# A graph attention kernel on one core: one batch's mask products and the copies into value blocks moved to the setup, and another listed order of the loop

## The chip, the cores and the metric

The kernel runs on one core of a Trainium2 chip, all in 32-bit floats. The metric is the device time of one execution in microseconds (us); lower is better. PE is the matmul engine (TensorE), DVE VectorE, ACT ScalarE, POOL GpSimd, SP SyncE, which issues most DMAs.

## The reference, cut to what matters

Sixteen batches (B) of 512 nodes with 512 features; a mask of 11 labels per pair of nodes, of which only the first 20 neighbours (NONGT) count; two directions d (the second with the mask transposed); 16 heads of 32.

```python
self_feat = concat([v, where(row_zero, 0, q)]) @ W_self.T + b_self
output = self_feat
for d in range(2):
    A = adj (d == 0) or its transpose (d == 1), first 20 neighbours
    cond, vb = A.sum(-1), A @ w_bias + b_bias
    kv = self_feat[:, :20]
    qh, kh = self_feat @ Wq[d].T + bq[d], kv @ Wk[d].T + bk[d]    # by head
    aff = where(cond > 0, einsum('bnhd,bmhd->bnhm', qh, kh) / sqrt(32), NEG) + vb
    w = softmax(aff)                                              # over the 20
    output += einsum('bnhm,bmf->bnhf', w, kv) through Wout[d] by head, + bout[d]
return v + relu(output)
```

## The kernel before, in words

**Setup (to about 97 us).** For all batches at once the setup works out the 20 neighbours' features, folds the query weights into the keys and the output weights into the values, and stores them in DRAM: keys in g_d (g1_d for batch 1), additive terms of the keys in cq_d, values in vw_d. The keys come in 22 bursts (n = 0 to 21, function keys): PE's matmuls, evictions into a stage "st" by ACT (L915) and DVE (L918), and, as soon as a stage is full, two stores by SP: a small one (L936, 76 KB) and a large one (L937, 1064 KB). There are four stage buffers, so a new stage waits for the stores of the fourth one before it. Between the bursts stand other pieces of the setup: masks and self_feat of batch 0 (L230), the clearing of the value blocks bd_d (L166, after bursts 8, 10, 12 and 14), and at n = 19 the two loads of batch 1's mask (adj, L141), after burst 19's stores. After the bursts come four loads of xn and the seeds.

**Value blocks.** For the last product (O) the values must lie in DRAM as blocks bd_d with zeros around them. Twelve DMAs (fill_block, L187, steps bl00 to bl11) copy rows of 128 bytes from vw_d into the cleared bd_d; each is 64 x 4 to 64 x 20 such rows. The loads vd (L162) read bd_d.

**The loop.** The loop is a software pipeline, unrolled. A table ORDER lists steps as "name±ahead"; the program goes through the table row after row (turn −1 to 17), and at turn t issues each step for batch t + ahead, if there is such a batch. Each engine gets its instructions in that order. The steps of one batch:
- loads (SP): Lx, Lxn, LG (keys), Lcq (L148, four DMAs), Lvd, Ladj; with PACE = 4 each load also waits for the instruction five earlier in the listing;
- seeds (ACT): sa writes the key terms cq into the bank pair ps_a (L476), sd the mask's sum into ps_d (L480), sc cq into ps_d again (L482);
- S1 to S7 (PE, L440): seven products of a Strassen-like scheme for the scores, 64 matmuls each, on sums y and z by POOL (Y and Z steps);
- t11 (ACT, L487) takes the first score tile out of ps_a, t12, f11 and so on (DVE, L492, L496) the others; then the softmax of four tiles: mx (DVE), sub (POOL L507), exp (ACT), sum, rec (DVE), nor (POOL L522), turn (DVE);
- F1 to F7 (PE, L292): seven products for the next batch's self_feat, on the banks ps_o; p and j (ACT, DVE) take them out;
- so (ACT, L533) puts self_feat into the banks ps_o, O0 and O1 (PE, L550) add the attention's output, oe (DVE, L560) ends it, st stores it;
- masks of the next batch: mul0 to mul10 (ACT, L363), one product of adj with the label's weight for each label, cnt (DVE, L369), flg (ACT), msum (DVE), sp (ACT).

For the last batch, other steps (P1 to P4, Oa to Oc) take the place of S and O.

S6 needs ps_a again after S1, so it waits until t11 has taken S1's result out. DMAs of SP and ACT are given completion counters, DMAHW0 to DMAHW7, in the order in which they are listed, whichever of the two engines issues them. In a list of the order, a row's "waits DMAHW3" means that this instruction waits until that counter has reached a value that the transfer given it before brings.

Of the kernel before, what the change touches and what calls it, by code (L numbers as in the profile page):

```python
# [14 lines left out]
NEG = -9000000000000000.0  # L15

ORDER = """
Z3+0 Z2+0 mul1+1 S2+0 mul2+1 Lx2+1 LG3+1 rec12-1 n22b-2 mul0+1 turn22-1 rb3-2 m22a-1 mul7+1 fu22+0
turn21-1 bl06+0 nor12-1 bl00+0 bl05+0 t11+0 S6+0 rb1-2 f11+0 bl02+0 P1+0 Lx3+1 Y3+0 u22a-1 turn12-1 e11+0
t12+0 mul9+1 bl09+0 mul10+1 bl11+0 so2-1 mul3+1 P4b-1 mul4+1 Lxn1+2 x22a-1 O0-1 Oa-1 mul6+1 O1-1 Lnz+1  # L20
k1+0 Z1+0 mul8+1 Lxn3+2 S7+0 Y4+0 mul5+1 sc+0 rb2-2 m22b-1 mx11+0 Ladj0+2 kv+1 oe2-1 flg+1 Lvd0+0 k2+0
oe3-1 rs0+2 S5+0 X1+1 sub11+0 LG1+1 oe0-1 F1+1 exp11+0 u22b-1 LG2+1 Lcq+2 ra0-2 v22a-2 rs2+2 t22+0 oe1-1
s22a-1 S4+0 bl01+1 msum+1 rs1+2 Z4+0 bl07+1 sum11+0 LG0+2 f22+0 Lx0+2 v22b-2 bl08+1 sA1-2 rs3+2 mx22+0
X2+1 f21+0 x22b-1 rm+2 p1+1 sp1+1 rec11+0 rb0-2 Ob-2 F6+1 bl04+1 bl10+1 nq+1 rst+2 P3+0 st1-1 ra3-1 bl03+1
nc+1 ra1-1 X3+1 Lxn0+3 sp0+1 S3+0 p2+1 P2+0 Ladj1+2 e21+0 mx21+0 sub22+0 exp22+0 Lvd3+0 nor11+0 nd+1 Oc-2
sub21+0 F7+1 rc0-2 exp21+0 X4+1 Lvd2+0 k3b+0 Lvd1+0 r22a-1 Lxn2+3 f12+0 F5+1 e12+0 sum22+0 p3+1 n22a-1
F2+1 F4+1 sd+1 st3-1 sA0-2 mx12+0 rec22+0 sum21+0 j3+1 sub12+0 rc2-2 nr+1 k0+1 st2-1 rec21+0 k3a+0 F3+1
turn11+0 j1+1 exp12+0 nor22+0 rc1-2 Lx1+2 p4+1 st0-1 s22b-1 nor21+0 sum12+0 sB0-2 j2+1 cnt+2 Y2+1 sa+1
S1+1 so3+0 P4a+0 rc3-2 ra2-1 sB1-2 so1+0 so0+0 r22b-1
"""  # L30
SOFT = 6
PACE = 4
# [3 lines left out]
def gat_kernel(  # L36
# [20 lines left out]
    nc = tc.nc  # L57
# [79 lines left out]
    def load_adj(b, i, ins=None):  # L137
        if i == 0:
            adjs[b] = load.tile([P, 4 * S, L], I32, tag="adj", name=f"adj{b}", bufs=1)
        to = adjs[b].rearrange("p (i v) l -> p i (v l)", i=2)  # L140
        behind(nc.sync.dma_start(to[:, i], adj[b, :, i]), ins)  # L141
# [29 lines left out]
    def blocks():  # L171

        bb = bd_d.rearrange("c b r e i g -> (c b) r e i g")
        vv = vw_d.rearrange("d c (b m) (e g) -> d (c b) m e g", m=NG, e=HL)
        for e in range(HL):
            for i in range(2):
                j = (e * S) // 32 + i
                for d in range(2):
                    lo = max(e * S + d * NG, 32 * j)
                    hi = min(e * S + (d + 1) * NG, 32 * j + 32)  # L180
                    if lo < hi:
                        m, r = lo - e * S - d * NG, lo - 32 * j
                        yield bb[:, r : r + hi - lo, e, i], vv[d, :, m : m + hi - lo, e]

    def fill_block(n):
        to, of = list(blocks())[n]
        nc.sync.dma_start(to, of)  # L187

    def ran(ins):
        done["all"].append(ins)  # L190
# [473 lines left out]
    with tc.tile_pool(name="setup", bufs=1) as sp, tc.tile_pool(name="ps_acc", bufs=4, space=PSUM) as acc["pool"]:  # L664
# [171 lines left out]
        with tc.tile_pool(name="setup_g", bufs=4) as sg:  # L836
# [137 lines left out]
            for n, runs in enumerate(bursts):  # L974
                for i in range(len(rest)):
                    if i < (4 if n == 0 else 1) or any(fc == 0 and (d, hg) == rest[0] for fc, hg, d, _, _ in runs):
                        key_rows(*rest.pop(0))
                keys(runs)
                for i in range(3 * n, min(3 * n + 3, 2 * C)):
                    bias_terms(i % 2, i // 2)  # L980
                if rest:
                    continue
                first = n if first is None else first
                for kind in plan[n - first] if n - first < len(plan) else ():
                    f, args = steps[kind].pop(0)
                    f(*args)
                if n == 5:
                    row_sums(0)
                if n in (8, 10, 12, 14):
                    clear_blocks(n // 2 - 4)  # L990
                if n == 7:
                    out_bias()
                if 8 <= n < 8 + C:
                    kv_bias(n - 8)
                if n == 12:
                    first_masks()
                if n == 13:
                    mask_count(0)
                if n == 14:
                    mask_flag(0)  # L1000
                    load_cq(0)
                if n in (14, 15):
                    for c in range(2):
                        self_flags(2 * (n - 14) + c)
                if n == 15:
                    mask_sum(0)
                    kv_copy(0)
                    row_sums(1)
                if n in (16, 17):
# [12 lines left out]
            while steps["s"]:  # L1022
                f, args = steps["s"].pop(0)
# [14 lines left out]
    with tc.manual_schedule():  # L1038
        banks = [bank(f"ps_o{c}", c) for c in range(C)]
        steps = {  # L1040
            "kv": kv_copy, "cnt": mask_count, "flg": mask_flag, "msum": mask_sum,
            "rm": row_mask, "rst": store_mask,
        }
        for c in range(C):
# [62 lines left out]

        def first(name):

            if name[:2] == "bl":  # L1110
                return (0,)
            if name in END:
                return (B - 1,)
            if name in NOT_END:
                return range(B - 1)
            if name[:2] in ("Lx", "rs", "rm", "La") or name == "Lnz":
                return range(3 if name[:3] == "Lxn" else 2, B)
            if name[0] in "FXpj" or name[:2] in ("LG", "Lc", "mu") or name in (
                "nd", "nc", "nq", "nr", "cnt", "flg", "msum", "sp0", "sp1", "kv"
            ):  # L1120
                return range(1, B)
            return range(B)
# [70 lines left out]
```

## Time and profile before

| | us |
|---|---|
| median of 3 runs | 596.72 (596.09 to 597.12) |
| profiled execution | 591.75, span 590.0 |
| loop's first score product (S1.0) starts | 97.38 |
| S7.1 (batch 1) starts | 146.94 |
| P1 of the last batch starts | 555.97 |

Rows of a timeline read: start us, duration us, engine, line, operation, out<-in, tile (partitions x elements), count, and in brackets the idle time before it and what ended it. "ACT s L487" as a releaser means that ACT's instruction of line 487 came last. Rows of DMA groups have the KB of one and the median us from issue to landing. Windows give, for a stretch, its length and each engine's busy time. q1 is the queue of SP's DMAs, q8 fetches PE's instructions. Line numbers are those of the kernel before; in the new kernel they are one lower up to about line 1000.

### The profile page before, as it was taken

The numbers are of one execution on the slowest core, as the hardware profiler recorded it, in microseconds if no ns is written. First come the engines' busy times: TensorE is split into PE (matmuls) and PEld (weight loads), VectorE is DVE, ScalarE is ACT, GpSimd is POOL, SyncE is SP. The second block draws the span as 40 slices with busy tenths as digits, with TensorE's granted clock in tenths as the row PEclk, the third lists the DMA queues.
The fourth block names the chain that finished last, engine by engine and source line by source line (L and its number), as shares of the span: only waits on it lengthen the run. The fifth ranks groups of instructions, "written<-read, shape, count | busy, mean of one in ns | idle before, by whom it ended". The sixth has DMA issues, their size and how long they took to land.

```text
span 590.0 us, 31439 instructions
## 1 busy us (share of the span) xinstructions
PE 560.5 (95%) x13980; PEld 437.4 (74%) x13980; DVE 433.7 (74%) x628; ACT 413.4 (70%) x890; POOL 427.8 (73%) x374
## 2 busy tenths in 40 slices
PE   8999999697999999998999999999999999999994
PEld 5443356586878787887888888877887777899983
DVE  0576571575878787877888787878787878788765
ACT  1344571786787878786878787878786868786622
POOL 2637945476687878786888887878787878888643
PEclk9999999898999999999999999999999999999997
DMA  8999999878766767766667776767666767652222
GB/s 292 380 396 370 322 316 373 222 180 239 190 222 180 222 192 227 199 209 159 228 196 223 195 222 192 220 172 228 188 215 183 219 185 212 202 175 87 70 93 73
DMA packets 102199, 127.88 MB, mean 217 GB/s; under 512 B 21457, under 2 KB 66545, under 8 KB 100017
## 3 DMA queue, kind: packets, MB, share of 16 engines
q1 hardware_dynamic: 100272, 123.73, 67.5%
q8 instruction: 110, 1.80, 1.3%
q0 software_dynamic: 672, 1.36, 1.0%
q10 hardware_dynamic: 1120, 0.79, 0.4%
q14 instruction: 25, 0.20, 0.1%
HBM read 85.97 MB, written 40.24 MB: 214 GB/s over the span
## 4 chain that ended last, share of the span: by engine, by line
PE 83%; POOL 5%; DMA 4%; issue 4%; DVE 2%; SPq 1%; ACT 1%; DVEq 0%; POOLq 0%; ACTq 0%
PE ps_o L292 30%; PE ps_a L440 22%; PE ps_d L440 15%; PE ps_o L550 8%; PE ps_k L798 3%; PE ps_a L456 1%; DMA ws_q<-in_wsT 1%; DMA vw_d<-v 1%; POOL st L924 1%; POOL cq_d L861 1%; SPq L148 1%; PE ps_kv L748 1%; DMA g_d<-st 1%; PE ps_d L456 1%; DMA xn<-in_xn 1%
## 5 line engine op out<-in xcount | busy, mean ns | idle before, releaser
L507 POOL TENSOR_TENSOR s<-s,top 128x640 f32<-128x640 f32 x63 | 80.5, 1277 | 68.8 <-DVE top L503 68.8
L363 ACT ACTIVATE prod<-adj,wb_sb 128x160 f32<-128x160 int32 x165 | 84.8, 590 | 13.3 <-POOL t L267 7.9
L522 POOL TENSOR_TENSOR s<-s,sum 128x640 f32<-128x640 f32 x63 | 79.8, 1278 | 12.3 <-DVE sum L518 12.1
L440 PE MATMUL ps_a<-y,z 128*32 128x152 f32 x1920 | 74.0, 301 | 13.1 <-issue 8.2
L292 PE MATMUL ps_o<-t,ws_s 128*32 128x246 f32 x1440 | 83.7, 370 | 0.0
L440 PEld LDWEIGHTS ps_a<-y,z 128*32 128x32 f32 x1920 | 64.1, 112 | 21.7 <-issue 18.7
L440 PE MATMUL ps_d<-g,z 128*32 128x152 f32 x1920 | 71.3, 293 | 0.3 <-issue 0.3
L511 ACT ACTIVATE s<-s 128x640 f32<-128x640 f32 x63 | 46.1, 732 | 36.1 <-POOL s L507 35.7
L292 PEld LDWEIGHTS ps_o<-t,ws_s 128*32 128x32 f32 x1440 | 56.0, 110 | 16.6
L440 PEld LDWEIGHTS ps_d<-g,z 128*32 128x32 f32 x1920 | 64.8, 110 | 2.8 <-issue 1.2
L292 PE MATMUL ps_o<-x,ws_v 128*32 128x246 f32 (+1 forms) x960 | 59.4, 373 | 0.3 <-issue 0.3
L560 DVE SCALAR_TENSOR_TENSOR o<-ps_o,x 128x512 f32<-128x512 f32 x60 | 38.4, 683 | 22.9 <-ACT cond L375 9.3
L492 DVE TENSOR_TENSOR s<-ps_a,both 128x640 f32<-128x640 f32 x45 | 37.1, 825 | 23.4 <-PE ps_a L440 23.1
L550 PE MATMUL ps_o<-wt,vd 32*32 32x256 f32 (+1 forms) x2176 | 49.3, 381 | 4.5 <-issue 2.6
L503 DVE TENSOR_REDUCE top<-s 128x32 f32<-128x640 f32 x63 | 51.2, 812 | 0.6
L515 DVE TENSOR_REDUCE sum<-s 128x32 f32<-128x640 f32 x63 | 50.2, 798 | 0.3 <-ACT s L511 0.3
L529 DVE STREAM_TRANSPOSE wt<-s 128x640 f32<-128x640 f32 x63 | 49.4, 802 | 0.0
L533 ACT COPY ps_o<-sf 128x512 f32<-128x512 f32 x64 | 36.6, 587 | 17.7 <-DVE sf L335 15.5
L292 PEld LDWEIGHTS ps_o<-x,ws_v 128*32 128x32 f32 x960 | 37.3, 110 | 13.3 <-issue 0.8
L550 PEld LDWEIGHTS ps_o<-wt,vd 32*32 32x32 f32 x2176 | 30.9, 105 | 19.3 <-issue 6.8
L496 DVE TENSOR_TENSOR s<-ps_d,s 128x640 f32<-128x640 f32 x45 | 36.9, 820 | 9.8 <-PE ps_d L440 9.2
L390 ACT COPY both<-add 32x160 f32<-32x160 f32 x128 | 41.1, 321 | 1.7
(283 smaller groups left out, 1228.0 us busy)
## 6 DMA issues: line engine op xcount, KB each, us to landing
g<-g_d SPq DMA_DIRECT2D x60, 304.0 KB, 3.8
g_d<-st SPq DMA_DIRECT2D x16, 1064.0 KB, 7.3
out_T<-o SPq DMA_DIRECT2D x60, 256.0 KB, 4.0
xn<-in_xn SPq DMA_DIRECT2D x56, 256.0 KB, 3.7
x<-in_xT SPq DMA_DIRECT2D x56, 256.0 KB, 3.6
adj<-in_adj SPq DMA_DIRECT2D x32, 440.0 KB, 4.6
vd<-bd_d SPq DMA_DIRECT2D x64, 64.0 KB, 3.4
nz<-nz_d SPq DMA_DIRECT2D x14, 256.0 KB, 3.8
```

Of the source, the lines that this page charges most:

```text
L292: nc.tensor.matmul(to[bass.ts(a, R), i] if wide else to[bass.ts(a, R), i, :, HK:], lhs, mov, start=wide and i == 0, stop=k == 1, skip_grou ...
L363: ran(nc.scalar.activation(new_prod(b)[:, :, l], adjs[b][:, :, l], AF.Identity, scale=wb_sb[:, l : l + 1]))
L390: ran(nc.scalar.copy(adds[b][bass.ts(2 * pg + hp, R), :, 2 * t : 2 * t + 2], add[bass.ts(2 * pg + t, R)]))
L440: nc.tensor.matmul(to[bass.ts(q, R)], rows[:, k, q // 2, bass.ds((2 * t + u) * R, R)], keys[:, k, q % 2], start=False, stop=k == 1, skip_g ...
L503: ran(nc.vector.tensor_reduce(tops[b, ij], flat(soft_tile(b, ij)), AX.X, ALU.max))
L507: ran(engine.tensor_sub(s, s, tops.pop((b, ij)).unsqueeze(2).to_broadcast([P, 4 * 2 * HL, NG])))
L511: ran(nc.scalar.activation(s, s, AF.Exp))
L515: ran(nc.vector.tensor_reduce(tops[b, ij], flat(soft_tile(b, ij)), AX.X, ALU.add))
L522: ran(engine.tensor_mul(s, s, tops.pop((b, ij)).unsqueeze(2).to_broadcast([P, 4 * 2 * HL, NG])))
L529: ran(nc.vector.transpose(wts[b][:, j, i], soft_t.pop((b, ij)).rearrange("p v h m -> p (v h m)")))
L550: nc.tensor.matmul(to, vds[b][r, j, e, i], w[:, :, bass.ts(block, 32)], start=False, stop=i == 1, skip_group_check=True,)
L560: ran(nc.vector.scalar_tensor_tensor(o, banks[q].rearrange("p (j n) -> p j n", j=2), 0.0, of_out(xs[b], hp, pg), ALU.max, ALU.add))
```

## The change

It has three parts. (1) The twelve copies into value blocks leave the loop and SP's queue: ACT issues them in the setup, three after each of the bursts 19, 20 and 21, and three after the last. (2) The two loads of batch 1's mask move from n = 19 to n = 15, ahead of three pairs of key stores on SP. (3) The table ORDER is replaced by another, which begins at another point of the row; batch 1's mask products, its F1 and most of batch 0's scores now stand in row −1. PE's steps in a steady row were F1 S4 F6 S3 F7 F5 F2 F4 F3 S1 S2 S6 O0 O1 S7 S5, and are F1 S4 S3 F6 F2 F7 F5 F4 F3 S1 S2 S6 O1 O0 S7 S5.

```diff
 ORDER = """
-Z3+0 Z2+0 mul1+1 S2+0 mul2+1 Lx2+1 LG3+1 rec12-1 n22b-2 mul0+1 turn22-1 rb3-2 m22a-1 mul7+1 fu22+0
...
+rs2+2 f22+0 flg+1 P3+0 Ladj0+2 oe1-1 ra0-1 sub11+0 fu22+0 p1+1 mx22+0 msum+1 Z4+0 n22a-1 st1-1 X2+1 S3+0
...
     def fill_block(n):
         to, of = list(blocks())[n]
-        nc.sync.dma_start(to, of)
+        nc.scalar.dma_start(to, of)
...
                     row_sums(1)
+                    load_adj(1, 0)
+                    load_adj(1, 1)
                 if n in (16, 17):
                     mask_spread(0, n - 16)
-                if n == 19:
-                    load_adj(1, 0)
-                    load_adj(1, 1)
+                if n > 18:
+                    for i in range(3):
+                        fill_block(3 * (n - 19) + i)
+            for n in range(9, 12):
+                fill_block(n)
             for j in range(4):
                 load_xn(2, j)
...
-        for n in range(len(list(blocks()))):
-            steps[f"bl{n:02d}"] = lambda b, n=n: fill_block(n)
...
-            if name[:2] == "bl":
-                return (0,)
```

ACT's queue from the end of the setup into the loop, before. L915 are evictions of the last key bursts, L480 and L476 the seeds sd and sa of batch 0, L363 the mask products of batch 1, L487 the step t11 of batch 0:

```order
L915 COPY st_1117<-ps_g(3, 3, 0, 0, 2)0_1107 128x2x8x19
L915 COPY st_1117<-ps_g(3, 3, 1, 1, 2)0_1139 128x2x8x19 [waits PE_49]
L480 COPY ps_d<-both_987 128x4x160 [waits DVE_49,PE_49,Activation_49]
L476 COPY ps_a<-cq_904 128x4x160 [waits DMAHW2_49,DMAHW1_49,DMAHW3_49,DMAHW0_49,Activation_49]
L363 ACTIVATE prod_1275<-adj_1104,wb_sb 128x160 [waits DMAHW6_49,DMAHW5_49,Pool_49]
L363 ACTIVATE prod_1275<-adj_1104,wb_sb 128x160 x3
L487 COPY s_11_1316<-ps_a 128x640 [waits DMASW2_49,DMASW3_49,DMASW1_49,DMASW4_49,DMASW0_49,DMASW5_49,PE_49,Activation_49]
```
The same place of the new kernel, a little shortened at its start (L914 evictions, L186 block copies, the first three of which stand ahead of these rows, L475 the seed sa):

```order
L914 COPY st_1120<-ps_g(3, 3, 0, 0, 2)0_1110 128x2x8x19
L186 DMA bd_d<-vw_d 64x20x32 [waits DMAHW2_49]
L186 DMA bd_d<-vw_d 64x4x32 [waits DMAHW4_49]
L186 DMA bd_d<-vw_d 64x16x32 [waits DMAHW5_49]
L914 COPY st_1120<-ps_g(3, 3, 1, 1, 2)0_1145 128x2x8x19 [waits PE_49]
L186 DMA bd_d<-vw_d 64x16x32 [waits DMAHW6_49]
L186 DMA bd_d<-vw_d 64x4x32 [waits DMAHW0_49]
L186 DMA bd_d<-vw_d 64x20x32 [waits DMAHW1_49]
L186 DMA bd_d<-vw_d 64x8x32 [waits DMAHW3_49]
L186 DMA bd_d<-vw_d 64x12x32 [waits DMAHW5_49]
L186 DMA bd_d<-vw_d 64x20x32 [waits DMAHW0_49]
L475 COPY ps_a<-cq_904 128x4x160 [waits DVE_49,PE_49]
```
Behind these stand L479 (sd), L486 (t11), L481 (sc) and only then the eleven L362 of batch 1. So t11 moved ahead of the mask products, and the evictions and the seeds moved behind block copies that wait on DMAHW counters. The same holds a row later: t11 of batch 1 stood behind four mask products of batch 2, and now stands ahead of all eleven.

SP's queue at the same time, before (L937 a large key store, L936 the small one ahead of it, L141 the loads of batch 1's mask):

```order
L937 DMA g_d<-st_886 128x2128 [waits DMAHW6_49]
L936 DMA g_d<-st_965 128x152 [waits DMAHW7_49,DVE_49,Activation_49]
L937 DMA g_d<-st_965 128x2128 [waits DMAHW0_49,DVE_49,Activation_49]
L936 DMA g_d<-st_1007 128x152 [waits DMAHW1_49,DVE_49,Activation_49]
L937 DMA g_d<-st_1007 128x2128 [waits DMAHW2_49]
L936 DMA g_d<-st_1050 128x152 [waits DMAHW3_49,DVE_49,Activation_49]
L937 DMA g_d<-st_1050 128x2128 [waits DMAHW4_49]
L141 DMA adj_1104<-in_adj 128x880 [waits DMAHW5_49]
L141 DMA adj_1104<-in_adj 128x880 [waits DMAHW6_49]
```
and in the new kernel (the stages st_965, st_1007, st_1050 and st_1117 of before are st_968, st_1010, st_1053 and st_1120 here):

```order
L936 DMA g_d<-st_886 128x2128 [waits DMAHW6_49]
L140 DMA adj_955<-in_adj 128x880 [waits DMAHW7_49]
L140 DMA adj_955<-in_adj 128x880 [waits DMAHW0_49]
L935 DMA g_d<-st_968 128x152 [waits DMAHW1_49,DVE_49,Activation_49]
L936 DMA g_d<-st_968 128x2128 [waits DMAHW2_49,DVE_49,Activation_49]
L935 DMA g_d<-st_1010 128x152 [waits DMAHW3_49,DVE_49,Activation_49]
L936 DMA g_d<-st_1010 128x2128 [waits DMAHW4_49]
L935 DMA g_d<-st_1053 128x152 [waits DMAHW6_49,DVE_49,Activation_49]
L936 DMA g_d<-st_1053 128x2128 [waits DMAHW0_49]
L935 DMA g_d<-st_1120 128x152 [waits DMAHW3_49,DVE_49,Activation_49]
L936 DMA g_d<-st_1120 128x2128 [waits DMAHW7_49,DVE_49,Activation_49]
```
The two loads moved ahead of three pairs of stores, and from st_1053 on the stores share the counters with ACT's block copies, which take numbers between them.

More of the change, by code (lines that the diff above doesn't have):

```diff
@@ L17 @@
 ORDER = """
-Z3+0 Z2+0 mul1+1 S2+0 mul2+1 Lx2+1 LG3+1 rec12-1 n22b-2 mul0+1 turn22-1 rb3-2 m22a-1 mul7+1 fu22+0
[L19 to L29, printed above, removed]
+rs2+2 f22+0 flg+1 P3+0 Ladj0+2 oe1-1 ra0-1 sub11+0 fu22+0 p1+1 mx22+0 msum+1 Z4+0 n22a-1 st1-1 X2+1 S3+0
+LG0+2 exp11+0 e12+0 sum11+0 ra3-1 f12+0 rec11+0 mx12+0 nd+1 nq+1 sub22+0 kv+1 X4+1 Lx0+2 X3+1 rs0+2 Lvd3+0
+Lvd2+0 Lvd1+0 F6+1 F2+1 p2+1 exp22+0 sum22+0 rb1-1 ra2-1 e21+0 rs3+2 k3a+0 Lxn2+3 nc+1 rs1+2 F7+1 v22b-2
+F5+1 st3-1 j1+1 rb3-2 nor11+0 f21+0 sub12+0 rb2-2 exp12+0 rm+2 p3+1 F4+1 rec22+0 sa+1 Ob-2 rst+2 P4a+0
+sA1-2 nr+1 Lxn0+3 mx21+0 k3b+0 sum12+0 j3+1 sp1+1 nor22+0 m22a+0 p4+1 F3+1 Oc-2 k0+1 S1+1 sp0+1 sd+1 Y2+1
+P4b+0 st0-1 rb0-2 Ladj1+2 sub21+0 s22b-1 rec12+0 S2+1 v22a-1 u22a+0 exp21+0 so3+0 Lcq+2 Lx1+2 turn11+0
+nor12+0 j2+1 t11+1 Z3+1 Z2+1 so2+0 sum21+0 m22b+0 rec21+0 sA0-2 turn12+0 P1+1 turn22+0 u22b+0 rc2-2 S6+1
+so1+0 Lx3+2 so0+0 k1+1 O1+0 f11+1 x22a+0 r22b-1 Lx2+2 s22a+0 rc0-2 nor21+0 Lxn3+3 sc+1 turn21+0 O0+0
+x22b+0 rc3-2 n22b-1 LG3+2 Y3+1 t12+1 Oa+0 mul3+2 mul7+2 Y4+1 S7+1 Lnz+2 P2+1 sB0-2 e11+1 cnt+2 oe3+0 LG1+2
+mx11+1 mul5+2 oe0+0 mul1+2 mul9+2 mul6+2 rc1-2 mul0+2 Z1+1 sB1-2 Lvd0+1 X1+2 mul2+2 mul10+2 oe2+0 S5+1
+Lxn1+3 k2+1 r22a+0 LG2+2 ra1+0 mul4+2 t22+1 F1+2 st2+0 S4+1 mul8+2
 """
```

## The prediction

> **What bounds the kernel now.** I read the page's shares first, then the windows by stage, PE's timeline at the loop's start, and then back through ACT and SP to what PE waits for there.
>
> ```profile
> PE 560.5 (95%) x13980; PEld 437.4 (74%) x13980; DVE 433.7 (74%) x628; ACT 413.4 (70%) x890; POOL 427.8 (73%) x374
> ```
> PE is busy for 95% of a span of 590.0 us, so what can be won is 29 us of idle PE and whatever PE did at a low clock. The windows (sum, PE, PEld, DVE, ACT, POOL, then granted clock, DMA share, GB/s) show where that lies: the whole first part of the loop, its two slow places, the thirteen steady rows, and the best of these.
>
> ```profile
> 97.38:146.94 49.56, 39.72 (x1000) 33.43 (x992) 26.89 (x34) 32.64 (x72) 31.20 (x26) 0.93 0.83 229
> 107.16:110.58 3.42, 2.83 (x48) 2.56 (x52) 0.82 (x1) 3.42 (x8) 0.00 (x0) 0.50 0.55 159
> 141.30:144.70 3.40, 3.40 (x76) 2.53 (x69) 2.30 (x4) 3.40 (x8) 3.40 (x4) 0.50 0.87 277
> 146.94:535.56 388.62, 382.18 (x10409) 318.01 (x10408) 316.15 (x429) 316.17 (x687) 315.46 (x260) 1.00 0.68 200
> 206.63:235.58 28.95, 28.95 (x805) 23.43 (x800) 24.33 (x33) 23.88 (x54) 23.96 (x20) 1.00 0.70 206
> ```
> From S7.1 on (146.94) PE is the bound: 382.18 of 388.62 us at full clock, with the others at some 316. Before that PE is idle for 9.8 of 49.56 us and gets half its clock twice. PE's timeline there, row by row:
>
> ```profile
> 97.38 2.25 PE L440 MATMUL ps_a<-g,sf 128*32 128x152 f32 x64
> 107.75 3.63 PE L440 MATMUL ps_a<-y,z 128*32 128x152 f32 x64 [5.08 <-issue]
> 112.42 0.85 PE L440 MATMUL ps_a<-y,z 128*32 128x152 f32 x20 [1.04 <-DVE s L492]
> 140.42 3.50 PE L440 MATMUL ps_a<-y,z 128*32 128x152 f32 x64 [3.73 <-ACT s L487]
> 143.85 3.17 PE L550 MATMUL ps_o<-wt,vd 32*32 32x256 f32 x128
> 262.31 2.75 PE L550 MATMUL ps_o<-wt,vd 32*32 32x256 f32 x128
> ```
> S1.0 starts at 97.38, S6.0 waits 5.08 us and S6.1 3.73 us. Each then runs at half clock (3.63 and 3.50 for 64 matmuls that take 2.25 elsewhere), and the O0 behind the second is slow too (3.17; 2.75 at 262.31). ACT shows why:
>
> ```profile
> 91.13 0.99 ACT L915 COPY st<-s_g(3, 3, 0, 0, 2)0_1107 128x608 f32<-128x608 f32 x2 [2.91 <-DMA g_d<-st]
> 92.75 0.42 ACT L915 COPY st<-s_g(3, 3, 1, 1, 2)0_1139 128x304 f32<-128x304 f32 x1 [0.63 <-PE s_g(3, 3, 1, 1, 2)0_1139 L900]
> 96.48 0.69 ACT L476 COPY ps_a<-cq 128x640 f32<-128x640 f32 x1
> 105.10 1.97 ACT L363 ACTIVATE prod<-adj,wb_sb 128x160 f32<-128x160 int32 x4 [7.93 <-POOL t L267]
> 106.98 0.67 ACT L487 COPY s<-ps_a 128x640 f32<-128x640 f32 x1
> ```
> The copy that S6.0 needs (t11.0, L487) stands behind four mask products of batch 1 (L363). These are put down to POOL, but POOL's t has nothing to do with them: what came at 105.0 is batch 1's adj, as SP's rows show (start, us of issue).
>
> ```profile
> 86.82 0.43 SPq L937 DMA_DIRECT2D g_d<-st  x1
> 87.39 0.34 SPq L936 DMA_DIRECT2D g_d<-st  x1
> 87.84 0.85 SPq L937 DMA_DIRECT2D g_d<-st  x1
> ...
> 89.97 1.19 SPq L937 DMA_DIRECT2D g_d<-st  x1
> ...
> 92.62 1.59 SPq L937 DMA_DIRECT2D g_d<-st  x1
> 94.27 2.44 SPq L141 DMA_DIRECT2D adj<-in_adj  x2
> ...
> 103.77 4.32 SPq L148 DMA_DIRECT2D cq<-cq_d  x4
> ```
> ```profile
> DMA packets 2970, 8.35 MB, mean 348 GB/s; under 512 B 377, under 2 KB 1601, under 8 KB 2326
> q1 hardware_dynamic: 2967, 8.30, 93.8%
> g_d<-st SPq DMA_DIRECT2D x5, 1064.0 KB, 8.6
> adj<-in_adj SPq DMA_DIRECT2D x2, 440.0 KB, 9.5
> g_d<-st SPq DMA_DIRECT2D x5, 76.0 KB, 7.2
> ```
> The last three rows are of 84 to 108 us, KB and median us from issue to landing. adj is issued at 94.27 and 95.5 and lands 9.5 later, at 103.8 and 105.0, through a queue that is 93.8% full of key stores.
>
> **The change, part by part.** *Gone from the start: 11.9 us.* t11.0 now stands ahead of batch 1's products, and t11.1 ahead of batch 2's, so neither waits for an adj. That removes 5.08 + 3.73 of waits, 3.63 − 2.25 = 1.38 and 3.50 − 2.25 = 1.25 of half clock, and 3.17 − 2.75 = 0.42 of O0: 11.86. The wait of 1.04 on DVE stays. What is late next for S6.0 are POOL's sums, the last piece of POOL in the chain of waits there:
>
> ```profile
> 103.82 1.19 POOL t L267
> ```
> They end by 105, before S1.0 starts by the next step. The eleven products (1.97 us for four, 5.4 in all) then run on an ACT that has 17 us idle in this stretch: nothing on PE's path. The 11.86 is an upper bound; the lower would be the first wait alone, 6.5.
>
> *New in the setup: twelve block copies on ACT.* Their own issues are cheap and their waits are not.
>
> ```profile
> L187 SPq DMA_DIRECT2D bd_d<-vw_d x12: 536/658/1601, 108.6 to 121.6; - x12
> ...
> DMA to landing us min/median/max: 3.0/3.6/5.0
> ```
> ```profile
> SPq L148 <- DMA adj<-in_adj: 2.2, 2, 1.3
> SPq L148 <- DMA g_d<-st: 2.0, 1, 2.0
> ```
> The last two rows decide the forecast. The cq loads read cq_d, which no adj and no g_d touches, and yet they wait for both: the first issues at 103.77, the moment the first adj lands. The transfers of SP and ACT share eight completion counters (DMAHW0 to 7 in the order) that go round in listed order, and an issue waits until the transfer eight places back has landed. On SP's end of the setup that cost PE nothing. On ACT it does, since ACT's evictions and the seeds of S1.0 are queued behind. By the listed order, third block waits for st_968's small store, fourth and fifth for the 1-MB stores of st_968 and st_1010, eighth for that of st_1053, twelfth for the eighth block.
>
> So in time: adj takes SP's place at 87.4, and the stores behind it issue 2.44 later than the rows above. st_968's small store: 87.39 + 2.44 + 7.2 = 97.0, then the third block issues (0.66), and the eviction that stood at 91.13 comes at 97.7. st_1010's big one: 89.97 + 2.44 + 8.6 = 101.0: the last eviction comes at some 102.5, not 92.75. st_1053's big one: 92.62 + 2.44 = 95.1, plus landing. Landings run from 4.2 to 9.6 in this stretch:
>
> ```profile
> L937 SPq DMA_DIRECT2D g_d<-st x5: 430/1055/1593, 86.8 to 98.2; - x5
> ...
> DMA to landing us min/median/max: 4.2/8.6/9.6
> ```
> I take 9.6, since 0.88 MB of adj now stand ahead of it: 104.7. Eighth block lands 3.6 later, 108.3; twelfth issues (0.66), then the seed (0.69): S1.0 at 109.7 in place of 97.38, **+12.3**. Bounds: 106 (landings of 7 and 3.0; the 4.2 was the first store into a queue not yet full) and 113 (9.6 and 5.0, and 2 us for stores that wait for their own counters), so +8.6 to +15.7. PE is then idle for most of 94 to 109.7, and after each of its two long waits of before it ran at half clock, for 1.25 and 1.38 more: **+1.3** (0 to 1.4). The blocks leave SP's queue in the loop (12 x 0.66 = 8 us of issue between 108.6 and 122.3); PE waited for none of these: nothing.
>
> *The steady rows: +0.5 (−2.3 to +2.5).* Six self_feat products in one row are the same matmuls, on the same four banks. PE's waits from 177 to 536:
>
> ```profile
> PE ps_a L440 <- issue: 3.2, 3, 1.6
> PE ps_o L550 <- issue: 2.6, 3, 1.0
> ...
> q8 instruction: 110, 1.80, 1.3%
> ```
> No wait on another engine is left to remove; 5.8 us are waits that the profile ascribes to nothing, in or right behind O0 and O1, of whose short matmuls PE uses up the most instructions per us (128 in 2.75, against 64 in 2.25). The 110 instruction fetches (16 KB each) fit them, and both orders have the same instructions ahead of each O. The Trainium skill ("Runtime: NRT & Kernel Launch", Instruction fetch mechanics) says that such fetches are mostly hidden, as a sequencer dispatches slower than its store fills; by it, these waits would come from the order and could go. No row here shows a fetch hidden or not, so this is a rival. What the new order can add is a wait for a sum that comes just late on POOL or DVE, which have about 5 us free in a row of 28.95: I put 0.04 us in each of 13 rows, and at most 0.19. *The tail* begins with P1, in the chain of waits:
>
> ```profile
> 555.97 4.13 PE ps_a L456 x117
> ```
> From there to the end of the span are 590.0 − 555.97 = 34.0 us, with the same steps in both: 0, ±0.7.
>
> The profiled execution took 591.75, the median of the runs is 596.72, so the 4.97 between them lie outside of these rows, and the difference is put on the median: 596.72 − 11.86 + 12.3 + 1.3 + 0.5 = **599.0 us**.
>
> **The rivals.** *The blocks are only issued (0.12):* if ACT's counters are free when it gets there, the twelve cost ACT 12 x 0.66 = 7.9 us, of which 2.91 + 0.63 lie in waits of ACT, so S1.0 comes 4.4 later: 596.7 − 11.9 + 4.4 + 0.5 = 589.8, faster. It decides if the eighth block issues before 98; against it are the two rows on SP.
> *The stores land sooner (0.18):* as the median, 8.6, and 3.0 for the block: S1.0 at 108.1 and no half clock on top, 596.1 to 597.4, about **no change**.
> *Blocks and stores share each DMA engine (0.08):* two blocks that go out beside a 1-MB store may have to let it pass. At the 348 GB/s of the window 1064 KB are 3.1 us, so the eighth block lands 6.7 after its issue: 602.1. For it: 3.0 to 5.0 were measured without such a store beside. The Trainium skill ("DMA: Bandwidth & Descriptors", Queues, rings and completion order) has a DMA engine turn between the queues packet by packet, and a block consists of many small rows. No trace of before has two busy queues.
> *The waits behind O go (0.05):* 599.0 − 5.8 = 593.2, if they are due to the order.
> *A wait in every row (0.03):* one like the 1.04 on DVE, thirteen times: +13.5, 612. The waits of the steady rows name no engine at all, against it.
>
> **How the numbers follow.** The forecast has 0.54, the rivals 0.12, 0.18, 0.08, 0.05 and 0.03. The range 594.5 to 603.5 takes in S1.0 from 106 to 113 (595.3 to 602.4) with a little of the steady rows' bounds, and the second and third rivals; it leaves out 0.12 + 0.05 + 0.03 = 0.2. About 0.2% (1.2 us) can be told from no change. Faster: 0.12 + 0.05 + 0.03 of the second rival = 0.20. Same: 0.15 of it and 0.05 of the forecast = 0.20. Slower: 0.49 + 0.08 + 0.03 = 0.60.
>
> **What would show it.** In the new profile, ACT's last two evictions (the line of 91.13 and 92.75) at about 98 and 102.5, block copies on ACT's queue that wait for g_d transfers, S1.0 at 109.7, half clock in it, no wait ahead of S6.0 and S6.1, S7.1 some 2 us later than 146.94, 13 rows in 389 us and a tail of 34. S1.0 before 104 would prove the step on counters wrong; rows that together differ by over 2.5 us would do so for the steady part.

## The result and the profile after

The changed kernel takes **622.38 us** (median of 4 runs, 620.68 to 624.02) against 596.84 us before (596.09 to 597.12): 1.043 times as long, 95% interval 1.0396 to 1.0463. Forecast were 599.0 us and a range up to 603.5. The direction was right; the forecast rise over the median of before was 2.3 us, the measured one 25.5.

The page of the profiled execution (620.68 us; before: 591.75):

```profile
span 618.9 us, 31420 instructions
PE 566.7 (92%) x13980; PEld 441.5 (71%) x13980; DVE 434.0 (70%) x628; ACT 416.3 (67%) x890; POOL 427.4 (69%) x374
q8 instruction: 110, 1.80, 1.2%
```
The span is 28.9 us longer. PE's timeline, from the last key burst to the first O, says where the start went:

```profile
104.04 0.62 PE L899 MATMUL s_g(3, 3, 1, 1, 2)0_1145<-khD,wq_sb 32*128 32x152 f32 x2 [10.78 <-ACT st L914]
...
109.63 1.87 PE L229 MATMUL ps_sf<-x,ws_v 128*32 128x246 f32 x32
115.32 3.87 PE L439 MATMUL ps_a<-g,sf 128*32 128x152 f32 x64 [3.82 <-ACT ps_a L475]
...
122.23 2.27 PE L439 MATMUL ps_a<-y,z 128*32 128x152 f32 x64
125.55 2.27 PE L439 MATMUL ps_a<-y,z 128*32 128x152 f32 x64 [1.04 <-DVE s L491]
...
151.82 2.76 PE L549 MATMUL ps_o<-wt,vd 32*32 32x256 f32 x128
```
S1.0 starts at 115.32 instead of 97.38 and runs at about half clock (3.87 us). After it nothing waits for a mask: S6.0 follows at 122.23 with no wait, and only the 1.04 on DVE is left. The windows of the first part and of the thirteen rows:

```profile
115.32:154.51 39.19, 38.15 (x997) 32.49 (x997) 25.29 (x32) 29.50 (x63) 26.73 (x23) 0.96 0.58 160
154.51:562.67 408.16, 386.79 (x10405) 324.75 (x10400) 316.14 (x430) 318.96 (x690) 316.51 (x262) 1.00 0.65 193
```
So the 28.9 us are +17.9 (S1.0 later) − 10.4 (39.19 instead of 49.56 from S1.0 to S7.1) + 19.5 (408.16 instead of 388.62 for the rows) + 1.8 (S7.14 to the end: 618.9 − 562.67 = 56.2 against 590.0 − 535.56 = 54.4). The tail from P1 on is as long as before (34.3 and 34.4 from the first matmul of P1).

Most of the last term is one wait of 1.66 us behind S7.14, like those in the rows. PE's waits in the rows are these, and the profile gives no engine for any of them:

```profile
PE ps_a L439 <- issue: 8.7, 8, 1.8
PE ps_o L549 <- issue: 5.7, 4, 1.9
PE ps_d L439 <- issue: 4.7, 7, 1.3
PE ps_o L291 <- issue: 1.9, 5, 0.6
```
That is 21.0 us, against 6.4 before, and PE's busy time in the rows grew by 4.6 (386.79 against 382.18 for the same work); the profile does not say why.

**ACT at the end of the setup.** Its queue shows the evictions (L914) and the seeds (L475, L479) between block copies:

```profile
89.68 13.20 ACTq L186 DMA_DIRECT2D bd_d<-vw_d  x3
102.99 0.68 ACT L914 COPY st<-s_g(3, 3, 0, 0, 2)0_1110 128x608 f32<-128x608 f32 x1 [13.43 <-DMA bd_d<-vw_d]
...
103.62 3.46 ACTq L186 DMA_DIRECT2D bd_d<-vw_d  x2
107.12 0.42 ACT L914 COPY st<-s_g(3, 3, 1, 1, 2)0_1145 128x304 f32<-128x304 f32 x1 [3.14 <-DMA bd_d<-vw_d]
107.15 7.32 ACTq L186 DMA_DIRECT2D bd_d<-vw_d  x6
114.57 0.70 ACT L475 COPY ps_a<-cq 128x640 f32<-128x640 f32 x1 [7.02 <-DMA bd_d<-vw_d]
```
The two evictions that were forecast for 98 and 102.5 come at 103.0 and 107.1, the seed at 114.57. The records of the DMA instructions say what held the copies between: the transfer whose counter a copy waits for, when that landed, when ACT issued the copy and how long the issue took, and when the copy landed (us):

```
copy      waits for               landed    issued  took    lands
sixth     first copy              106.52    106.55  0.53   109.54
eighth    st_1053's large store   106.24    107.85  0.68   113.77
twelfth   eighth copy             113.77    113.79  0.68
third     st_968's small store     97.41     97.43  5.45   107.50
fifth     st_1010's large store   103.14    103.62  2.78   108.93
tenth     st_1120's small store   108.70    109.86  2.93   116.14
```
The first three rows are the chain that ends last: ACT waits for the first copy, which landed 16.8 us after its issue at 89.68, then goes through the sixth copy, the eviction and the seventh to the eighth, and the twelfth waits for the eighth to land. The last three rows are long issues beside it: from 89.7 to 114.5 the twelve issues took 17.3 us in all, and ACT's waits ahead of issues 7.0. These issues ended just before the landings of 106.52 and 113.77 (at 106.40, and at 113.47 with the eleventh copy), so either of the two would have held ACT nearly as long. Why they were long no run shows.

The group of the block copies (ns to issue, then us from issue to landing):

```profile
L186 ACTq DMA_DIRECT2D bd_d<-vw_d x12: 537/670/5450, 89.7 to 113.8; - x12
...
DMA to landing us min/median/max: 3.0/6.0/16.8
```

### The profile page after: what moved, and what is told of

It reads as the page before. It is cut to its first block, busy times and chain, and to the rows that moved or that the text cites. A ratio compares the mean times of both kernels' runs of the same rounds, so it can differ in the third digit from the quotient of the medians.

```text
span 618.9 us, 31420 instructions
## 1 busy us (share of the span) xinstructions
PE 566.7 (92%) x13980; PEld 441.5 (71%) x13980; DVE 434.0 (70%) x628; ACT 416.3 (67%) x890; POOL 427.4 (69%) x374
## 4 chain that ended last, share of the span: by engine, by line
PE 82%; DMA 6%; issue 5%; DVE 2%; POOL 2%; ACT 1%; SPq 0%; ACTq 0%; DVEq 0%; POOLq 0%
PE ps_o L291 29%; PE ps_a L439 21%; PE ps_d L439 15%; PE ps_o L549 7%; DMA bd_d<-vw_d 4%; PE ps_k L797 3%; DMA ws_q<-in_wsT 1%; PE ps_a L455 1%; DMA g_d<-st 1%; PE ps_v L874 1%; POOL st L923 1%; PE ps_kv L747 1%; PE ps_d L455 1%; ACT st L914 1%; POOL rx L216 0%
## 5 line engine op out<-in xcount | busy, mean ns | idle before, releaser
L291 PE MATMUL ps_o<-t,ws_s 128*32 128x246 f32 x1440 | 86.2, 371 | 0.7 <-issue 0.7
L362 ACT ACTIVATE prod<-adj,wb_sb 128x160 f32<-128x160 int32 x165 | 80.6, 586 | 0.0
L439 PE MATMUL ps_d<-g,z 128*32 128x152 f32 x1920 | 73.6, 293 | 4.8 <-issue 4.7
L291 PEld LDWEIGHTS ps_o<-t,ws_s 128*32 128x32 f32 x1440 | 58.4, 110 | 18.8 <-issue 1.6
L510 ACT ACTIVATE s<-s 128x640 f32<-128x640 f32 x63 | 46.3, 735 | 30.1 <-POOL s L506 29.7
L291 PE MATMUL ps_o<-x,ws_v 128*32 128x246 f32 (+1 forms) x960 | 61.4, 373 | 1.2 <-issue 1.2
L336 ACT COPY sf<-ps_o 128x492 f32<-128x492 f32 x30 | 17.1, 570 | 61.8 <-PE ps_o L291 53.1
L514 DVE TENSOR_REDUCE sum<-s 128x32 f32<-128x640 f32 x63 | 51.0, 809 | 10.7 <-ACT s L510 10.6
L502 DVE TENSOR_REDUCE top<-s 128x32 f32<-128x640 f32 x63 | 49.4, 785 | 0.1
L291 PEld LDWEIGHTS ps_o<-x,ws_v 128*32 128x32 f32 x960 | 40.0, 110 | 11.7 <-issue 1.5
L549 PEld LDWEIGHTS ps_o<-wt,vd 32*32 32x32 f32 x2176 | 30.5, 104 | 24.0 <-issue 11.5
L408 POOL TENSOR_TENSOR z<-sf,z 128x512 f32<-128x512 f32 x30 | 39.0, 1299 | 5.6 <-DVE sf L238 4.5
```

The lines of the kernel that those rows point to most:

```text
L291: nc.tensor.matmul(to[bass.ts(a, R), i] if wide else to[bass.ts(a, R), i, :, HK:], lhs, mov, start=wide and i == 0, stop=k == 1, skip_grou ...
L362: ran(nc.scalar.activation(new_prod(b)[:, :, l], adjs[b][:, :, l], AF.Identity, scale=wb_sb[:, l : l + 1]))
L408: ran(nc.gpsimd.tensor_sub(t, one, two))
L439: nc.tensor.matmul(to[bass.ts(q, R)], rows[:, k, q // 2, bass.ds((2 * t + u) * R, R)], keys[:, k, q % 2], start=False, stop=k == 1, skip_g ...
L502: ran(nc.vector.tensor_reduce(tops[b, ij], flat(soft_tile(b, ij)), AX.X, ALU.max))
L510: ran(nc.scalar.activation(s, s, AF.Exp))
```

## The experiments

Two causes were to be tested, each against a rival. For the start, *counters*: ACT waits in its queue for the transfers that hold the copies' completion counters (rival: the key stores themselves come later, as the mask's loads stand ahead of them). For the rows, *fetch*: PE waits for its instructions, whose fetches are held up by other transfers, and the new table crowds eight loads around O, where PE uses up its instructions fastest (rival: the new order of the steps makes PE wait for other engines). The second came up only with this trace. Of the DMA records of the changed kernel, four fetches of PE's queue (16 KB each) and the wait of PE behind each, in us:

```
fetch starts, ends   PE idle from, to    at matmul number
186.15  187.06       186.89  188.72       2999
250.62  251.66       251.41  253.04       4653 = 2999 + 13.0 x 127.2
405.23  406.20       405.75  407.69       8596 = 4653 + 31.0 x 127.2
469.25  470.14       469.98  471.77      10250 = 8596 + 13.0 x 127.2
```
PE stops at multiples of 127 matmuls (with their 127 weight loads; one fetch of 16 KB each) and starts again 1.4 to 1.7 us after the fetch has ended. Counted from when PE enters the block of instructions before, the fetch begins about 0.96 us later in the rows of before and 1.87 in those of after (means over some 80 fetches; over 2 us in about 10% and 48% of them). At their pace, a block of 127 matmuls of S lasts 4.1 us, one of O 2.7, one of F 6.6. So a fetch that begins 1.87 us late, takes 1.1 (the mean of the 110) and leaves 1.4 until PE goes on needs an estimated 4.4 us, more than a block of S gives; with 0.96 it is 3.5. The share of the DMA engines' time that other transfers took, by tenths of a row from the start of O (mean over 13 or 14 rows, worked out from the same records):

```
kernel before      0.67 0.50 0.71 0.73 0.39 0.75 0.77 0.57 0.63 0.66
changed kernel     0.90 0.68 0.80 0.60 0.71 0.55 0.15 0.49 0.68 0.81
loads spread       0.27 0.08 0.61 0.54 0.64 0.82 0.79 0.96 0.90 0.37
copies at O        0.95 0.76 0.55 0.52 0.56 0.61 0.84 0.73 0.56 0.93
```
In the changed kernel it is 0.90 while O runs and 0.15 in the middle of the F products. The two lower rows are experiments told below. In each comparison the kernel before ran on the same chip, with medians from 593.9 to 596.3 us; the changed kernel ran only for the result. The rows of one kernel differ between executions: thirteen rows took 388.6 us in the profile of before, and 389.8 and 395.1 in those of two experiments that leave its loads in the rows as they are (the old table with the new setup, and the mask's loads alone). A difference of up to some 7 us in the rows of two profiles is no effect by itself.

**The copies on SP** (changed kernel):

```diff
     def fill_block(n):
-        nc.scalar.dma_start(to, of)
+        nc.sync.dma_start(to, of)
...
-                if n > 18:
-                    for i in range(3):
-                        fill_block(3 * (n - 19) + i)
-            for n in range(9, 12):
-                fill_block(n)
             for j in range(4):
                 load_xn(2, j)
+            for n in range(12):
+                fill_block(n)
```


> The new kernel with one edit: the twelve block copies are issued by SP, all of them behind the four xn loads at the end of the setup, and not by ACT between the bursts. Theory (counters): the late start of the loop is ACT waiting in its queue for the transfers that hold the copies' counters. Then S1.0 starts at 97 to 100 instead of 115.3, without the 1.6 us of half clock, S7.1 at about 137 instead of 154.5, and the median falls by 16 to 18, to 604 to 606. Rival (the stores themselves come later, because the mask's loads now stand ahead of them): S1.0 stays behind 108, the median above 614. Both expect the steady rows to stay at 31.4 us.

Measured: median 613.1 us (603.15 to 615.73), ratio to before 1.0206 (1.0085 to 1.0327). S1.0, in the timeline of its profiled execution (603.15 us):

```profile
98.65 2.25 PE L439 MATMUL ps_a<-g,sf 128*32 128x152 f32 x64
...
135.23 2.27 PE L439 MATMUL ps_a<-y,z 128*32 128x152 f32 x64 [2.52 <-POOL z L408]
137.44 2.76 PE L549 MATMUL ps_o<-wt,vd 32*32 32x256 f32 x128
140.13 1.24 PE L439 MATMUL ps_a<-y,z 128*32 128x152 f32 x32
```
The start is back at 98.65, at full clock, with the mask's loads where the change put them: it was the copies on ACT, not the stores. That ACT waited for counters is read from the table above; this run takes the long issues off ACT together with the waits, so it does not part the two. S7.1 came 3 us later than expected, since S6.1 now waits 2.52 us for POOL. The rows stay slow (405.9 us). The median fell by 9, not 16, a miss: the profiled execution was the shortest of four, and what made the others (611.0 to 615.73 us) longer no profile shows.

**The loads spread** (changed kernel, table only; the steps of PE, ACT, DVE and POOL stay in their order):

```diff
-... F6+1 F2+1 p2+1 exp22+0 ... so0+0 ... Lx3+2 ... Lx2+2 ... Lxn3+3 ... LG3+2 ... LG1+2 ... Lxn1+3 ... LG2+2 ...
+... F6+1 Lx1+2 F2+1 LG3+2 p2+1 exp22+0 Lx2+2 ... F7+1 LG1+2 ... st3-1 Lx3+2 ... nor11+0 Lxn3+3 ... F4+1 LG2+2 ... Lxn0+3 Lxn1+3 ...
```


> The new kernel with eight loads (Lx1 to Lx3, LG1 to LG3, Lxn1, Lxn3) moved in the table from the stretch of S1 to S5 around O to the stretch of the six F products; all compute steps stand as they did. Theory (fetch): PE's unexplained waits in the steady rows are instruction fetches held up by the crowd of loads. Then the rows go from 31.4 to 29.4 to 29.8, the waits from 21 us to under 5, and the median falls by 16 to 24, to 598 to 606, with S1.0 still at about 115. Rival (the new order of the compute steps makes PE wait for other engines): the rows stay at 31 or more, the median within 4 us of 622.

Measured: 602.42 us (600.38 to 603.94), ratio to before 1.0131 (1.0053 to 1.0208) instead of 1.043: 8.6 us over the kernel before, where the changed kernel was 25.5 over it. The window of the thirteen rows, and PE's waits in them:

```profile
154.28:545.05 390.77, 383.18 (x10405) 320.28 (x10400) 316.02 (x430) 319.73 (x690) 316.99 (x262) 1.00 0.65 200
```
```profile
PE ps_a L439 <- issue: 4.8, 5, 1.4
PE ps_o L549 <- issue: 1.9, 3, 0.8
PE ps_d L439 <- issue: 0.5, 1, 0.5
```
With the same steps in the same order the rows take 390.8 us instead of 408.2, and the waits 7.2 instead of 21.0. S1.0 stays at 115.1. The rival for the rows has fallen. The median came as expected; the rows (30.1 us each) and the waits stayed just above what was expected.

**Both edits** (the two diffs above together). 

> Both edits together: copies on SP behind the xn loads, and the eight loads moved to the F stretch. Theory (counters and fetch, independent of each other): S1.0 at 97 to 100, rows at 29.4 to 29.8, median 580 to 588, faster than the kernel before by 9 to 16 us. Rival (either cost is something else): above 600.

Measured: 594.8 us (593.29 to 597.05), ratio 0.9997 (0.996 to 1.0033): no different from before, and a miss by some 7. S1.0 at 98.67, but S2.1 waits 2.18 us for a seed whose cq loads stand behind the copies on SP, S7.1 comes at 142.0, the rows take 30.4 us each, and 11.5 us of fetch waits are left from the loop's start on.

**The old table with the new setup** (the changed kernel, with before's table less its bl steps):

```diff
-rs2+2 f22+0 flg+1 P3+0 Ladj0+2 oe1-1 ra0-1 sub11+0 fu22+0 p1+1 ...
+Z3+0 Z2+0 mul1+1 S2+0 mul2+1 Lx2+1 LG3+1 rec12-1 n22b-2 mul0+1 ...
```


> The new setup with the old table: block copies on ACT in the setup, batch 1's mask loaded at n = 15, the steps in the order of before. Theory (the two costs are separate, the first belongs to the copies, the second to the table): S1.0 at 114 to 116 with half clock, no wait of S6.0 for the mask, rows at 29.6 to 30.0 as before, median 606 to 612. Rival (the late start needs the new table, or the slower rows come from the new setup): S1.0 near 97, or rows above 31.

Measured: 603.43 us (602.99 to 606.04), ratio 1.0154 (1.009 to 1.0218). PE's S1.0, and the window of the rows:

```profile
117.30 4.28 PE L439 MATMUL ps_a<-g,sf 128*32 128x152 f32 x64 [6.07 <-ACT ps_a L475]
```
```profile
157.55:547.33 389.78, 383.00 (x10406) 319.47 (x10401) 316.13 (x429) 316.87 (x690) 316.76 (x261) 1.00 0.67 200
```
The two costs come apart: the late start belongs to the copies, the slow rows to the table. It came out 3 us better than expected, since S6.1 had no wait either: from S1.0 to S7.1 were 40.3 us here, almost as with the new table. So with a start this late, what was won behind it did not need the new order of ACT's steps: the second half of batch 2's mask landed at 143.49, 5.8 us later than in the kernel before (137.71), but the loop started 19.9 us later.

**More traffic at one place** (kernel before, four copies of 256 KB more in each row, from an input to a tensor that nobody reads):

```diff
+    more_d = dram.tile([B, C, P, N], F32, name="more_d")
...
+    def more(b):
+        for c in range(C):
+            nc.sync.dma_start(more_d[b, c], xT[b, bass.ts(c, P)])
...
-... S6+0 rb1-2 ...
+... S6+0 more+0 rb1-2 ...
```


> The kernel before with four extra copies of 256 KB in each row (from an input to a DRAM tensor that nobody reads), issued by SP right behind S6, that is, just ahead of O. No step of the computation moves. Theory (fetch): the copies hold up PE's instruction fetches where the blocks of instructions are shortest, so the unexplained waits of PE rise from 6.4 us to 14 to 25, and the median by 8 to 20 us. Rival (such waits belong to an order of the steps): they stay at 6 to 8 us, and the median rises by under 3.

Measured: 636.55 us (630.61 to 640.45), ratio 1.0643 (1.055 to 1.0736): 40 us more than before, twice the upper end of what was expected. The rows and PE's waits in them:

```profile
153.07:582.43 429.36, 395.82 (x10405) 335.31 (x10400) 316.42 (x429) 316.03 (x687) 315.24 (x260) 0.98 0.70 213
```
```profile
PE ps_a L445 <- issue: 14.4, 7, 3.6
PE ps_o L555 <- issue: 12.0, 9, 3.8
PE ps_d L445 <- issue: 6.5, 4, 2.4
```
The old order of the steps, with traffic just ahead of O, has 33.5 us of the same waits. The rest of the 40.7 us that the rows grew by is PE's busy time (395.82 against 382.18), at a granted clock of 0.98 on average. The same copies in the F stretch ("more+0" behind F7+1): 

> The same four extra copies, but issued behind F7, in the stretch of F products, where a block of instructions lasts longest. Theory (fetch): the waits of PE rise by under a third of what they do with the copies ahead of O, the median by 0 to 5 us. Rival (any extra traffic costs the same, wherever it stands): as much as with the copies ahead of O.

Measured: 607.38 us (604.32 to 617.19), ratio 1.017 (1.0092 to 1.0247).

```profile
PE ps_o L555 <- issue: 8.6, 8, 2.3
PE ps_a L445 <- issue: 6.1, 6, 2.1
```
With the smaller groups the waits are 17.8 us: 11 more than before, where the copies ahead of O add 27. The median rose by 11 against 40. More than the expected third in the waits, and above the 5 us: the place decides most of it, but not all.

**The mask's wait alone** (kernel before):

```diff
-Z3+0 Z2+0 mul1+1 S2+0 ... bl05+0 t11+0 S6+0 ...
+Z3+0 Z2+0 t11+0 mul1+1 S2+0 ... bl05+0 S6+0 ...
...
                     row_sums(1)
+                    load_adj(1, 0)
+                    load_adj(1, 1)
...
-                if n == 19:
-                    load_adj(1, 0)
-                    load_adj(1, 1)
```


> The kernel before with two edits: t11 stands ahead of the next batch's mask products in the table, and batch 1's mask is loaded at n = 15. Block copies and everything else as before. Theory: this is the part of the change that was priced at 11.9 us. S1.0 at 97 to 99, from there to the first O 36.5 us instead of 46.5, the steady rows as before, the median 8 to 12 us under the kernel before. Rival (the waits come back elsewhere, as ACT gets late with the masks): under 4 us.

Measured: 602.83 us (596.84 to 607.49), ratio 1.0086 (1.0042 to 1.013): within 2% of before, and not faster: a miss. PE at the first O:

```profile
136.43 2.27 PE L440 MATMUL ps_a<-y,z 128*32 128x152 f32 x64 [1.17 <-POOL z L409]
143.41 4.59 PE L550 MATMUL ps_o<-wt,vd 32*32 32x256 f32 x128 [4.71 <-DVE wt L529]
```
S6.0 and S6.1 no longer wait for a mask, but O0 waits 4.71 us for DVE's turn and runs at about half clock. The turn is late by the same mask: ahead of it in DVE's queue stands the count of batch 2's mask (cnt, L369), which waits 8.88 us until the second half of that mask lands at 139.66. So the wait for the mask went from ACT to DVE. Each row takes 30.7 us with t11 at its new place. With seven loads moved as well:

```diff
-... S2+0 ... Lx2+1 LG3+1 ... Lx3+1 ... Lxn1+2 ... Lnz+1 ... Lxn3+2 ... Lx1+2 ...
+... F6+1 Lx1+2 ... Lxn0+3 Lxn1+3 ... S3+0 Lx2+2 ... F7+1 LG3+2 ... F5+1 Lx3+2 F2+1 Lxn3+3 ... F3+1 Lnz+2 ...
```


> The kernel of the run before this one (t11 first, mask of batch 1 early) with seven loads (Lx1 to Lx3, LG3, Lxn1, Lxn3, Lnz) moved from the stretch around O into that of the F products. Theory (fetch): the unexplained waits fall from 6.4 to under 3 us, the rows from 29.7 to about 29.3, the median 12 to 17 us under the kernel before. Rival (the remaining waits are not due to traffic): no better than without the moved loads.

Measured: 602.76 us (595.37 to 603.97), ratio 1.0079 (1.0037 to 1.0121): no better, a miss for the theory as a recipe. Its rows took 30.5 us and had 9.9 us of such waits, against 9.0 without the moved loads. Only the mask's loads at n = 15, in the kernel before (the diff above without its first two lines): 

> The kernel before with only batch 1's mask loaded at n = 15. Theory: the first wait is the mask's: S6.0 starts without its wait of 5.1 us and at full clock, S6.1's wait of batch 2's mask stays at 3 to 5 us; S7.1 comes 5 to 7 us sooner, the median falls by 3 to 7 us. Rival (another wait takes its place, since SP's later work is held up by the same stores): S7.1 less than 2 us sooner.

Measured: 595.97 us (593.84 to 600.18), ratio 1.0034 (1.0007 to 1.0062). The rival's result:

```profile
141.53 4.28 PE L440 MATMUL ps_a<-y,z 128*32 128x152 f32 x64 [6.68 <-ACT s L487]
```
S6.0's wait is gone, and S6.1 waits 6.68 us in place of 3.73, for t11 behind batch 2's mask products; that mask landed at 138.82.

**The copies further back.** The changed kernel with the copies as steps of row −1 on SP, behind batch 1's cq loads, and five loads spread:

```diff
-        nc.scalar.dma_start(to, of)
+        nc.sync.dma_start(to, of)
...
+        for n in range(len(list(blocks()))):
+            steps[f"bl{n:02d}"] = lambda b, n=n: fill_block(n)
...
-... Lcq+2 Lx1+2 turn11+0 ...
+... Lcq+2 bl00+1 bl01+1 ... bl11+1 turn11+0 ...
```


> The new kernel with its table, the twelve block copies on SP in row -1 behind batch 1's cq loads, and five loads (Lx1 to Lx3, LG3, Lxn3), those that stand ahead of O, moved to the F stretch; LG1, LG2 and Lxn1 stay behind O. Theory (counters and fetch): S1.0 at 97 to 99, from there to the first O 36.5 to 37.5 us, with no wait for cq, unexplained waits of 5 to 10 us, median 4 to 10 us under the kernel before. Rival (the time saved at the start is given back by fetches): no more than 2 us under it.

Measured: 601.92 us (600.14 to 602.93), ratio 1.0109 (1.0044 to 1.0174), a miss: 40.6 us from S1.0 to the first O, with a wait of 3.1 for POOL, and 16.5 us of fetch waits in the rows. The next run moves the three loads that stayed behind O as well and is 7 us shorter. With all eight spread: 

> The same with all eight loads moved to the F stretch, as in the run with both edits, but with the copies behind batch 1's cq loads. Theory: as there, without its wait of 2.2 us for cq: median 2 to 6 us under the kernel before. Rival (the wait moves on to another load behind the copies): within 2 us of it.

Measured: 595.11 us (591.83 to 597.88), ratio 1.001 (0.9983 to 1.0037). S7.1 starts at 137.39, 9.6 us sooner than before, and the next row gives 8.6 of it back (38.9 us to S7.2, against 30.3). PE shows on what:

```profile
141.37 1.24 PE L440 MATMUL ps_a<-y,z 128*32 128x152 f32 x32 [2.74 <-issue]
147.69 3.19 PE L292 MATMUL ps_o<-x,ws_v 128*32 128x256 f32 x32 [3.01 <-DVE o L560]
172.19 0.45 PE L440 MATMUL ps_a<-y,z 128*32 128x152 f32 x4 [1.00 <-issue]
```
Fetch waits are 3.7 us of it. F1 waits 3.01 for oe, which frees its banks, and then runs at a low clock (3.19 us; 1.9 elsewhere). On DVE, oe stands behind the count of batch 2's mask, which waits 8.17 us until that mask lands at 143.63: once more the mask's wait, by way of DVE. This one without the copies:

```diff
             if name[:2] == "bl":
-                return (0,)
+                return ()
```


> The run with all eight loads spread and the copies behind cq, with the twelve block copies left out altogether, so that the values' blocks stay zero and the output lacks the attention's part. Theory (what the early start wins is given back to transfers, since the copies and all loads behind them crowd the first row): S7.1 at 136 to 138 as with the copies, and from there to S7.2 30 to 32 us instead of 38.9, the median 588 or less. Rival (the crowd is the loads of the first rows themselves): still over 35 us from S7.1 to S7.2.

Measured: 589.34 us, with runs from 578.33 to 592.07, and no interval. 33.3 us from S7.1 to S7.2: 5.6 of the 8.6 went with the copies, in a profiled execution that was the slowest of its four (592.07). Without the copies batch 2's mask lands at 132.29, before DVE needs it, and the wait for oe is gone. What is left over the 30.3 us of before are fetch waits (0.97, 0.61 and 1.55).

**Less traffic** (kernel before):

```diff
+            if name in ("st0", "st1", "st2", "st3"):
+                return ()
```


> The kernel before with the output stores st0 to st3 left out (all batches but the last are not written), 1 MB less in each row of some 6 MB, and nothing else changed. Theory (fetch): less traffic, so the unexplained waits fall from 6.4 us to under 4, and the thirteen rows from 388.5 us to 381 to 386. Rival (such waits stand at fixed places of the instruction stream and do not depend on traffic): 6 to 7 us, 387 to 390.

Measured: 593.73 us (592.27 to 597.6), ratio 0.9993 (0.9962 to 1.0024), rows 393.2 us, 8.3 us of waits. A miss: taking 1 MB a row away elsewhere than at O gained nothing.

No version was found that beats the kernel before by more than its runs scatter.

## Why the prediction was wrong, point by point

**Right in its number, not in its reason: what goes from the start.** Priced at 11.86, less 1.3 for half clock: 10.6. From S1.0 to S7.1 10.4 us went, 1.6 of half clock in S1.0 counted. The reason given was that t11 no longer stands behind the mask products. It is true of ACT, but the number was luck: with the old table and the same late start 9.3 us went too, because the loop came later by more than the masks did. With an early start other waits take the mask's place, for POOL, for a seed's cq loads, or for DVE, where the count of the mask stands ahead of the turn or of oe. From S1.0 to S7.1 the new table then takes 38.6 to 43.3 us in the four runs that keep the copies, and where it takes 38.6 the row behind gives most of the gain back; the old table with t11 first takes 48.0, against 49.6.

**Right in its mechanism, mis-sized: the step "st_1053's big one: 92.62 + 2.44 = 95.1, plus landing … Eighth block lands 3.6 later"**. Moving the copies to SP brought S1.0 back from 115.3 to 98.7. The term was +12.3 (bound 15.7) and measured +17.9. Three pieces were too small. The store landed at 106.24, not 104.7. ACT came to the eighth block only at 107.85, 1.6 later, because the sixth block waits for the first, which the sum left out and which landed 16.8 us after its issue. And the eighth block landed 5.9 us after its issue, not 3.6. "Their own issues are cheap" did not hold either: 0.66 us was taken for each, and four took 1.25 to 5.45. The "rival" of blocks that share each DMA engine with stores, given 0.08, was part of what happened. Its evidence, packets that started in slices of 2 us, from the DMA records:

```
us          SP's queue (q1)   ACT's queue (q10)
 96 to  98        198               200
 98 to 100        143               143
102 to 104        105               114
110 to 112         88                82
104 to 106        136              2228
```
In the first four slices SP's queue kept the DMA engines busy for 96 to 98% of the time, and ACT's queue started about as many packets as SP's, whatever their size: ACT's packets are rows of 128 bytes, SP's were 3.7 to 8.5 KB on average. In the last slice SP's queue was busy for 28%, and ACT's rows went more than ten times as fast. The Trainium skill ("DMA: Bandwidth & Descriptors", Queues, rings and completion order) says that a DMA engine goes round the queues that have work, a packet at a time; the equal counts agree with that, though the trace's packets are single rows and do not show how many the engine takes in one turn. So here a copy of many small rows beside large stores moved at the stores' pace, and my 3.6 us, taken from rows without such stores, was the wrong one to lean on.

**Wrong: "The steady rows: +0.5 (−2.3 to +2.5)".** They cost 19.5. The step that failed was "both orders have the same instructions ahead of each O", from which I took it that the fetches would cost the same. The waits were fetches, as I had read them, and as many (110); but what a fetch takes depends on the traffic at that moment, and I looked only at the new order of the compute steps, not at where the loads fell in the row. Moving eight loads took 17 of the 19.5 away; adding traffic at that place to the old order made its rows 41 us longer. In the profiles of three more kernels with the eight loads moved the gain is smaller: the last twelve rows take 362.1 to 366.0 us, against 359.5 in the first such run, 373.4 in the changed kernel and 358.3 in the kernel before. The Trainium skill ("Runtime: NRT & Kernel Launch", Instruction fetch mechanics) says that such fetches are mostly hidden. By their number this trace agrees: some 82 fetches fall in the thirteen rows, and PE has 8 such waits there before and 24 after. But these cost 6.4 and 21.0 us. The rival that I drew from it, waits that go with the new order, had the wrong sign.

**Right: the tail,** 34.3 us in place of 34.4 from P1's first matmul. What the place on SP's queue in the loop is worth by itself no run shows.

**Open.** Why the waits of the kernel before stay at 6 to 8 us when stores are taken away, and do not fall when seven loads are moved with t11 first; why kernels with the same loads in the rows differ by some us of these waits; why PE's busy time in the rows of the changed kernel grew by 4.6 us; and why some issues of block copies took up to 5.45 us.

## What to carry to other kernels

Before moving DMAs to another engine's queue, follow each one's completion counter to the transfer before it: on an engine that also computes, everything behind it waits for that landing. When a table of steps is re-ordered, look at where its loads fall beside the stretch where PE eats its instructions fastest (many short matmuls), not only at the compute steps. And a wait that leaves the start of a pipeline is won only if the transfers that the next steps need can come sooner too: here 8.6 of 9.6 us were given back within a row. When a step is moved ahead of the wait for a load, look at every other engine whose queue has a step that needs the same load: here the mask held DVE once it no longer held ACT.

## What the hardware showed that was not expected

- PE's wait for a fetch of 16 KB can be longer than 3 us under load (3.8 at most, in the run with copies ahead of O), and such waits are not labelled: they appear as "issue", at multiples of 127 matmuls.
- While SP's queue of large stores was busy for 96 to 98%, ACT's queue of 128-byte rows started about as many packets as it did: 198 and 200, 143 and 143, 105 and 114, 88 and 82 in slices of 2 us.
- 1 MB of extra copies a row costs 40 us in all ahead of O and 11 in the stretch of the F products, though the share of the DMA engines over the rows, 0.70 and 0.76, is lower in the first.
